# Score products of a 32-head attention on 64-row tiles of the TensorE array instead of all 128 rows with zeros

## The chip, the core and the metric

The kernel runs on one core of a Trainium2 chip. The core has a TensorE (PE in the profile) that multiplies matrices, a VectorE (DVE), a ScalarE (ACT), a GpSimd (POOL) and a SyncE (SP), which here only issues transfers. The engines run side by side, each through its own queue in order, and wait for each other on semaphores. TensorE works in two instructions: a weight load (LDWEIGHTS, engine "PEld" in the profile) puts one operand into the array, and a matmul (MATMUL, "PE") streams the other operand through it, a column at a time, into PSUM. The array has 128 rows, over which the product is summed, and 128 columns; an instruction can also be addressed to a part of it, called a tile, for which the program gives a size (rows by columns) and a position.

The metric is the device time of one execution in microseconds (us); less is better.

## What is computed

Two transformer layers on an input of 4 x 512 x 512, each an attention and a feed-forward part with layer norms and residuals. The change touches the attention of layer 0:

```python
NUM_HEADS, HEAD_DIM = 32, 16          # HIDDEN = 512, one key/value head for all query heads
q = (hidden_states @ Wq).reshape(b, s, NUM_HEADS, HEAD_DIM)
kv = hidden_states @ Wkv
k, v = (kv[..., :HEAD_DIM], kv[..., HEAD_DIM:])
scores = jnp.einsum('bqhd,bkd->bhqk', q, k) * scale
bias = slopes[:, None, None] * (pos[None, None, :] - pos[None, :, None])
scores = jnp.where(causal[None, None], scores + bias[None], -jnp.inf)
attn = jax.nn.softmax(scores, axis=-1)
out = jnp.einsum('bhqk,bkd->bqhd', attn, v).reshape(b, s, h)
return out @ Wo
```

After it come a quantized linear layer, a second attention (32 heads of 128, 8 key/value heads, rotary positions) and a feed-forward part with octonion products. The change does not touch these.

## The kernel before

The program has three stages on one core. Stage A is the attention of layer 0 with, woven into it, the projections, the layer norms and the quantized linear layer that follow it (classes `A1` and `A2`). Stage B is the second attention (`phase_b`), stage C the last feed-forward part (`C`). The matmuls at lines 422 to 483 lie in stage A alone; the last of them starts at 670 us of 2411.6.

Products of float32 precision are made from pieces: every operand is split into a rounded part h and a rest l, both of the type float32r, and three products hh, hl, lh are summed (`mm3_gen`, lines 159 to 161). For the scores of layer 0 the three products fit into one contraction, since a head has only 16 dimensions. One head takes 64 rows: 16 rows q_h against k_h, 16 rows q_l against k_h, 16 rows q_h against k_l, and 16 rows for the position bias, the block mask and, in row 58, the row maximum. Two heads share the 128 rows:

- `QS[m]` (m = 0 to 3, eight heads each) is 128 x 4 x 512. Rows 0 to 63 hold four heads, rows 64 to 127 four others (`two` = 0 and 1 in the code).
- `KS[b]` (one for each batch b) is 128 x 2 x 512. Copy `two` = 0 holds the keys in rows 0 to 63 and zeros in rows 64 to 127; copy `two` = 1 the other way round. A product over all 128 rows with copy `two` gives the scores of the head in that half; the zeros take the other head out.

The softmax is done in two passes over the scores. In the first, `max_tile` (lines 409 to 433) computes scores with 128 queries as output rows and up to 512 keys as columns, and the DVE takes the negative row maximum (line 430) into `mn`. Line 422 makes the first query block of two heads at once: it streams both copies of `KS` (2 x 128 keys) against weights from all 128 rows of `QS`. Line 426 makes one head's query block 1, 2 or 3 with 256, 384 or 512 keys. `max_end` transposes `mn` (line 439) and sends the maxima into row 58 (and 122) of `QS` by DMA (line 446). In the second pass, `exp_tile` (lines 449 to 473) computes the scores again, transposed, with 128 keys as output rows and four heads x 128 queries as columns (line 467); the ACT takes the exponential (line 470), the POOL clears what lies above the diagonal (line 472). `pv` multiplies by the values (line 483): its four matmuls for four heads go to column tiles of 32 columns each, 128 rows x 32 columns at column 0, 32, 64 and 96, in float32, which the profile shows as two instructions each (x8 for four).

The score matmuls write into few buffers: three PSUM banks `ps` (`psS`) for the maxima and two `pt` (`psT`) for the exponentials; two more banks `mm` serve the projections. A matmul waits until the DVE or the ACT has read the bank it writes.

`run` (line 561) goes over 128 units u; in unit u it records the three or four maxima matmuls of head u % 8, and the exponentials of unit u - 12, with other work (generators that are stepped in between: `front`, `qproj`, `o_piece`, `posts` of `A2`). The order in which the instructions are issued is not the recorded one: a scheduler that runs at build time and estimates durations arranges them, with the exponentials raised in priority by 100. It is thus built anew when an instruction is changed.

Two other matmuls of stage A use a part of the array: the bias row of the linear layer (line 818, two rows, `matmul(y, one, b0)`, tile of 32 rows x 128 columns, float32r) and the transpose of a 32-row tile (line 354). The transpose of the maxima at line 439 has a tile of 128 rows x 32 columns at column 0.

Of the kernel before, what the change touches and what calls it, by code (L numbers as in the profile page):

```python
# [215 lines left out]
class A1:  # L216
# [192 lines left out]
    def max_tile(self, b, m, j, q):  # L409

        nc = self.nc
        two, pr = j // 4, j % 4
        ks = self.KS[b]
        if j == 0 and q == 0:
            assert (b, m) in self.queries
            self.mn = self.sm.tile([128, 8, 4], F32, name="mn", tag="mn", bufs=2)
        ps = self.psS.tile([128, 512], F32, name="ps", tag="ps")
        qs = self.QS[m][:, pr]
        todo = []
        if q == 0 and j < 4:  # L420
            p = ps[:, 256:512].rearrange("p (i t) -> p i t", i=2)
            nc.tensor.matmul(p, qs[:, :128], ks[:, :, :128], start=True, stop=True)
            todo += [(j, 0, p[:, 0]), (j + 4, 0, p[:, 1])]
        qb = q + 1
        p = ps[:, :128 * (qb + 1)]
        nc.tensor.matmul(p, qs[:, bass.ts(qb, 128)], ks[:, two, :128 * (qb + 1)], start=True, stop=True)  # L426
        for jj, qb, p in todo + [(j, qb, p)]:
            nk = 128 * (qb + 1)
            jk = self.jp.tile([128, 512], BF, name="jk", tag="jk")
            nc.vector.tensor_tensor_reduce(  # L430
                out=jk[:, :nk], in0=p, in1=self.c.mask[:, 384 - 128 * qb:512],
                scale=-1.0, scalar=3e38, op0=ALU.add, op1=ALU.min,
                accum_out=self.mn[:, jj, qb:qb + 1])
# [15 lines left out]
    def exp_tile(self, v, q):  # L449

        nc, c = self.nc, self.c
        b, m, two, kb = v // 32, v // 8 % 4, v // 4 % 2, v % 4
        qb = kb + q
        if qb > 3:
            return
        ks = self.KS[b][:, two]
        if qb == 3:
            self.exped = v + 1
        if q == 0:
            assert v < self.maxed  # L460
            self.pe[v] = self.pp.tile([128, 4, 512 - 128 * kb], F32, name="pe", tag=f"pe{kb}")
        self.turn = (self.turn + 1) % 5
        if self.u >= 32 * B + 2 and self.turn < 3:
            ps = self.psS.tile([128, 512], F32, name="ps", tag="ps").rearrange("p (h t) -> p h t", h=4)
        else:
            ps = self.psT.tile([128, 4, 128], F32, name="pt", tag="pt")
        nc.tensor.matmul(ps, ks[:, bass.ts(kb, 128)], self.QS[m][:, :, bass.ts(qb, 128)],  # L467
                         start=True, stop=True)
        e = self.pe[v][:, :, bass.ts(q, 128)]
        nc.scalar.activation(e, ps, AF.Exp)  # L470
        if q == 0:
            nc.gpsimd.affine_select(out=e, in_=e, pattern=[[0, 4], [1, 128]], compare_op=ALU.is_ge,  # L472
                                    fill=0.0, base=0, channel_multiplier=-1)
# [921 lines left out]
```

## Time and profile before

| | |
|---|---|
| median of 3 runs | 2411.65 us (2411.24 to 2412.7) |
| the profiled execution's own time | 2413.31 us |
| its span from first to last instruction | 2411.6 us |
| mean granted TensorE clock | 0.981 of full speed |

| engine | busy us of the span | share | instructions |
|---|---|---|---|
| PE (matmul) | 2301.8 | 95% | 11606 |
| PEld (weight load) | 1794.2 | 74% | 11606 |
| DVE | 1573.0 | 65% | 4631 |
| ACT | 1076.9 | 45% | 2404 |
| POOL | 1190.3 | 49% | 1387 |

The matmuls of lines 422, 426 and 467 are 64, 384 and 320 in number; line 483 has 1024 recorded. Busy time of a PE row runs from the moment the matmul is issued to its modelled end, so rows of successive matmuls overlap, and a start-to-start distance tells more of the cost of one matmul than its duration does. The time that a matmul waits for its operands or its bank is shown as idle time of PEld or PE before it, with the instruction that ended the wait. "issue" there means that nothing in the profile explains the wait. The granted clock is what the TensorE's throttle let through, as a share of full speed.

### The profile page before, as it was taken

What the parts mean: (1) busy time and instruction counts of PE and PEld (TensorE: products, weight loads), DVE (VectorE), ACT (ScalarE), POOL (GpSimd) and SP (SyncE); (2) the same over time, 40 slices, a digit from 0 to 9 for tenths busy, and PEclk for the clock granted to TensorE, in tenths of its full rate; (3) what the DMA queues carried; (4) which work ended last, traced back from release to release, by engine and by line L of the source; (5) the groups of instructions that cost most, each with busy time, mean ns of one, the idle gap of its engine ahead of it and who ended that gap; (6) DMA issues with size and microseconds to landing.
All of it is one profiled execution on the core that took longest, in us unless ns stands there. A gap on an engine that the chain in (4) does not pass through costs nothing.

```text
span 2411.6 us, 35873 instructions
## 1 busy us (share of the span) xinstructions
PE 2301.8 (95%) x11606; PEld 1794.2 (74%) x11606; DVE 1573.0 (65%) x4631; ACT 1076.9 (45%) x2404; POOL 1190.3 (49%) x1387
## 2 busy tenths in 40 slices
PE   6899889988889999999999999999999999999998
PEld 4566455555557788888888888888888888878886
DVE  7766656555356777777777767777777778764443
ACT  3555445545543344444444444444444445453332
POOL 3323333434343676566566566666656667522221
PEclk8899899999999999999999999999999999999999
DMA  8845434343367432233122222232222222041000
GB/s 183 238 145 181 98 92 111 89 106 110 94 188 207 135 103 75 88 101 102 66 88 105 70 88 97 79 106 70 88 97 79 91 85 79 14 127 57 31 27 18
DMA packets 158558, 241.54 MB, mean 100 GB/s; under 512 B 26738, under 2 KB 91506, under 8 KB 149540
## 3 DMA queue, kind: packets, MB, share of 16 engines
q1 hardware_dynamic: 141748, 202.42, 27.9%
q0 software_dynamic: 14768, 35.92, 5.3%
q8 instruction: 93, 1.52, 0.3%
q10 hardware_dynamic: 1856, 0.92, 0.2%
q14 instruction: 93, 0.76, 0.1%
HBM read 183.17 MB, written 63.92 MB: 102 GB/s over the span
## 4 chain that ended last, share of the span: by engine, by line
PE 84%; issue 4%; DMA 4%; DVE 3%; POOL 2%; ACT 2%; SPq 1%; ACTq 0%; POOLq 0%; DVEq 0%
PE mm L182 11%; PE mm L184 11%; PE mm L183 11%; PE pt L989 6%; PE mm L159 3%; PE pt L467 3%; PE po L483 3%; PE po L1002 3%; PE po L1003 3%; PE mm L161 3%; PE po L1004 3%; PE mm L160 3%; PE ps L969 3%; PE ps L970 3%; PE ps L971 3%
## 5 line engine op out<-in xcount | busy, mean ns | idle before, releaser
L980 POOL TENSOR_TENSOR s<-s,r 128x384 f32<-128x384 f32 (+3 forms) x512 | 359.6, 722 | 130.0 <-DVE r L979 119.7
L977 ACT ACTIVATE s<-s,mn 128x384 f32<-128x384 f32 (+3 forms) x512 | 286.0, 560 | 223.8 <-DVE mn L973 215.9
L863 POOL TENSOR_TENSOR rp_a<-rp_a,rp_b 128x512 f32<-128x512 f32 x155 | 200.3, 1292 | 262.3 <-DVE rp_b L862 247.5
L992 ACT CAST ph<-pt 128x512 fp32r<-128x512 f32 x320 | 181.7, 586 | 295.5 <-PE pt L989 287.8
L430 DVE CUSTOM_DVE_ANT_0 jk<-ps,mask 128x384 bf16<-128x384 f32 (+3 forms) x512 | 227.5, 483 | 81.2 <-PE ps L426 72.1
L993 DVE TENSOR_TENSOR pl<-pt,ph 128x512 fp32r<-128x512 f32 x320 | 216.5, 686 | 43.4 <-ACT ph L992 40.4
L973 DVE CUSTOM_DVE_ANT_0 s<-ps,mask 128x384 f32<-128x384 f32 (+2 forms) x384 | 203.1, 552 | 37.7 <-PE ps L971 19.5
L470 ACT ACTIVATE pe<-pt 128x512 f32<-128x512 f32 x307 | 174.4, 600 | 97.0 <-PE pt L467 92.7
L989 PE MATMUL pt<-ident,s 128*128 128x128 f32 x1280 | 214.1, 272 | 0.7 <-POOL s L980 0.5
L182 PE MATMUL mm<-xh,w_h 128*128 128x512 f32 x512 | 205.4, 401 | 2.1 <-DVE rp_b L862 1.9
L182 PE MATMUL mm<-w_h,oh 128*128 128x512 f32 x512 | 203.7, 398 | 0.7 <-ACT oh L1008 0.7
L184 PE MATMUL mm<-xh,w_l 128*128 128x512 f32 x512 | 203.6, 398 | 0.0
L183 PE MATMUL mm<-xl,w_h 128*128 128x512 f32 x512 | 202.1, 395 | 0.0
L183 PE MATMUL mm<-w_l,oh 128*128 128x512 f32 x512 | 201.7, 394 | 0.0
L184 PE MATMUL mm<-w_h,ol 128*128 128x512 f32 x512 | 200.3, 391 | 0.0
L989 PEld LDWEIGHTS pt<-ident,s 128*128 128x128 f32 x1280 | 164.7, 140 | 46.1 <-POOL s L980 1.1
L865 POOL TENSOR_TENSOR ql<-rp_a,qh 128x512 fp32r<-128x512 f32 x124 | 160.5, 1294 | 49.6 <-ACT qh L864 49.6
L472 POOL TENSOR_SCALAR_AFFINE_SELECT pe<-pe 128x512 f32<-128x512 f32 x128 | 82.5, 647 | 195.7 <-ACT pe L470 195.1
L859 DVE TENSOR_TENSOR rp_a<-mm,cosq 128x512 f32<-128x512 f32 x128 | 88.4, 691 | 119.6 <-PE mm L184 94.3
L426 PE MATMUL ps<-KS,QS 128*128 128x256 f32 (+2 forms) x384 | 132.7, 384 | 19.2 <-DVE mn L430 18.7
L108 POOL TENSOR_TENSOR ln_rs<-ln_ve,mhalf 128x1 f32<-128x1 f32 x112 | 63.8, 575 | 173.0 <-DVE ln_ve L106 145.5
L1008 ACT CAST oh<-po 128x512 fp32r<-128x512 f32 x128 | 74.5, 582 | 166.1 <-PE po L1004 165.9
(359 smaller groups left out, 5872.5 us busy)
## 6 DMA issues: line engine op xcount, KB each, us to landing
xh<-xt SPq DMA_DIRECT2D x32, 1024.0 KB
xl<-xt SPq DMA_DIRECT2D x32, 1024.0 KB
vh<-v SPq DMA_DIRECT2D x32, 256.0 KB
vl<-v SPq DMA_DIRECT2D x32, 256.0 KB
raw<-in_a_wo SPq DMA_DIRECT2D x32, 256.0 KB
w_h<-in_a_wo POOLq DMA_DIRECT2D x32, 256.0 KB, 3.2
m_d<-t_d SPq DMA_DIRECT2D x192, 42.5 KB
QS<-qh_d SPq DMA_DIRECT2D x62, 128.0 KB
```

The source lines that it names most:

```text
L182: nc.tensor.matmul(ps, lh(k), rh(k), start=(j == 0), stop=False)
L183: nc.tensor.matmul(ps, lh(k), rl(k), start=False, stop=False)
L184: nc.tensor.matmul(ps, ll(k), rh(k), start=False, stop=(j == n - 1))
L430: nc.vector.tensor_tensor_reduce(out=jk[:, :nk], in0=p, in1=self.c.mask[:, 384 - 128 * qb:512], scale=-1.0, scalar=3e38, op0=ALU.add, op1= ...
L470: nc.scalar.activation(e, ps, AF.Exp)
L863: eng.tensor_tensor(a, a, r, ALU.add)
L973: nc.vector.tensor_tensor_reduce(out=s[:, :nk], in0=ps[:, :nk], in1=mask, scale=-1.0, scalar=3e38, op0=ALU.add, op1=ALU.min, accum_out=mn)
L977: nc.scalar.activation(s[:, :nk], s[:, :nk], AF.Exp, bias=mn, scale=-1.0, accum_out=l)
L980: nc.gpsimd.tensor_tensor(s[:, :nk], s[:, :nk], r.to_broadcast([128, nk]), ALU.mult)
L989: nc.tensor.transpose(pt[:, j], PS[u, qb, j][:, bass.ts(kb, 128)], c.ident)
L992: nc.scalar.copy(ph, pt)
L993: nc.vector.tensor_tensor(pl, pt, f(ph), ALU.subtract)
```

## The change

The score matmuls of lines 426 and 467 contract over the 64 rows that hold something, instead of over all 128. Both operands are cut to rows 64 x `two` to 64 x `two` + 63, and the matmul is addressed to the array's tile of 64 rows x 128 columns at row 0 or row 64. That makes 704 matmuls, 352 in each half. Line 422, whose weights hold two heads, stays on 128 rows. No instruction is added or taken away, the shapes of outputs, the buffers and the order in which the program records its instructions stay the same; the scheduler arranges them anew.

```diff
@@ max_tile
         qb = q + 1
         p = ps[:, :128 * (qb + 1)]
-        nc.tensor.matmul(p, qs[:, bass.ts(qb, 128)], ks[:, two, :128 * (qb + 1)], start=True, stop=True)
+        rows = slice(64 * two, 64 * two + 64)
+        nc.tensor.matmul(p, qs[rows, bass.ts(qb, 128)], ks[rows, two, :128 * (qb + 1)],
+                         start=True, stop=True, tile_position=(64 * two, 0))
         for jj, qb, p in todo + [(j, qb, p)]:
@@ exp_tile
-        nc.tensor.matmul(ps, ks[:, bass.ts(kb, 128)], self.QS[m][:, :, bass.ts(qb, 128)],
-                         start=True, stop=True)
+        rows = slice(64 * two, 64 * two + 64)
+        nc.tensor.matmul(ps, ks[rows, bass.ts(kb, 128)], self.QS[m][rows, :, bass.ts(qb, 128)],
+                         start=True, stop=True, tile_position=(64 * two, 0))
         e = self.pe[v][:, :, bass.ts(q, 128)]
```

In the issue order of the built programs, up to the last matmul of line 483, the tile size changes from one matmul to the next 299 times before the change and 598 times after it. The 704 matmuls then stand in 253 groups with no matmul of another tile size in between: 81 groups of one, 51 of two, 40 of three, 26 of four, 39 of five and 16 of six to eight. Of the 451 neighbours within a group, 350 lie in the same half of the array and 101 in different halves.

## The prediction

> **What bounds the kernel now.** I first read the page's shares and the chain that ended last, to see which engine sets the end.
>
> ```profile
> span 2411.6 us, 35873 instructions
> PE 2301.8 (95%) x11606; PEld 1794.2 (74%) x11606; DVE 1573.0 (65%) x4631; ACT 1076.9 (45%) x2404; POOL 1190.3 (49%) x1387
> PE 84%; issue 4%; DMA 4%; DVE 3%; POOL 2%; ACT 2%; SPq 1%; ACTq 0%; POOLq 0%; DVEq 0%
> ```
>
> TensorE is the chain for 84% of the span. The change lies in stage A, so I read the busy time of three stretches of it.
>
> ```profile
> 100.00:300.00 200.00, 186.15 (x1046) 118.16 (x1045) 127.77 (x502) 106.63 (x203) 62.00 (x80) 0.96 0.54 151
> 300.00:500.00 200.00, 179.40 (x971) 115.73 (x971) 116.85 (x466) 95.26 (x169) 72.53 (x107) 0.96 0.41 98
> 500.00:700.00 200.00, 177.06 (x943) 111.34 (x942) 98.06 (x348) 98.92 (x176) 76.55 (x107) 0.95 0.41 125
> ```
>
> The columns are the stretch, its length, busy PE, PEld, DVE, ACT, POOL, then granted clock, DMA share and GB/s. PE is busy for 542.6 of 600 us; the next engine, DVE, for 342.7. So PE sets the pace of stage A too, with some waits for others. What PE time is added here mostly reaches the end, since stage B can't start before it and is PE-bound itself. The question is then only what the 704 matmuls cost PE.
>
> **What a matmul costs on part of the rows.** No 64-row tile stands in this trace. The nearest row is line 818: same type float32r, same 512 columns, on a tile of 32 rows, between matmuls on all rows. This is the timeline of PE there (start, duration, engine, line).
>
> ```profile
> 375.39 0.39 PE L160 MATMUL mm<-w_l,x1h 128*128 128x512 f32 x1
> 375.62 0.39 PE L161 MATMUL mm<-w_h,x1l 128*128 128x512 f32 x1
> 375.93 0.50 PE L818 MATMUL mm<-b,one 2*128 2x512 f32 x1
> 376.36 0.50 PE L467 MATMUL pt<-QS,KS 128*128 128x512 f32 x1
> 376.79 1.06 PE L483 MATMUL po<-pe,vx 128*32 128x512 f32 x8
> ```
>
> Read the distances between starts. L160 to L161 is 0.23 us: 512 columns in a stream. L161 to L818 is 0.31 (the median of the 13 such steps in the trace's start times is 0.318): the tile size changes, and the load waits until L161 is through, 0.09 more. L818 to L467 is 0.43: again 0.09 for leaving, and 0.11 because its weight load started with it (durations 0.50 against 0.39). Without both, L818 takes the same 0.23 as 128 rows do. So fewer rows save nothing by themselves, and **a change of row tile costs 0.09 us for emptying the array plus 0.11 us for a load that no matmul covers**, 0.20 in all.
>
> A change of tile size isn't always dear:
>
> ```profile
> 413.37 0.39 PE L161 MATMUL mm<-wo_h,otl 128*128 128x512 f32 x1
> 413.60 0.27 PE L439 MATMUL mm<-ident,mn 128*32 128x128 f32 x1
> 413.62 0.48 PE L467 MATMUL pt<-QS,KS 128*128 128x512 f32 x1
> 413.94 0.28 PE L422 MATMUL ps<-KS,QS 128*128 128x256 f32 x1
> ```
>
> L439 is a transpose on 128 rows and 32 columns at column 0. It enters 0.23 after L161, as if nothing changed, and L422 starts 0.34 after it; a whole-array transpose and L467 would take 0.11 and 0.23, the same. So this change of column tile is free, and the change of rows at L818 is not. I take L818's price for 64 rows, because there as here the rows differ, and keep L439's price, zero, as the lower bound. The Trainium skill ("TensorEngine Tiling (Array Packing)", Key Properties) says that changing the tiling mode drains the TensorE. By that rule L439 would pay too; the row contradicts it, so the rule alone would not decide. By the rule every one of the added changes pays.
>
> **The sum, part by part.** Removed: nothing in number; the 704 matmuls keep their 0.23, 0.17 or 0.12 us for 512, 384 and 256 columns (start-to-start medians 0.232, 0.178 and 0.120).
>
> Added: changes of tile size. The built order has 598 against 299, so 299 more. Line 422 alone, left on 128 rows in the midst of them, stands in front of a 64-row matmul 64 times. Emptying: 299 x 0.09 = 26.9 us. Uncovered loads of 128 columns: arrivals at a tile of 128 columns go from 161 to 454 (253 at 64 rows, 185 at 128 rows, 16 at 32 rows), 293 x 0.108 = 31.6 us (0.108 is the step from 0.228 to 0.336, the common distance after a change). Arrivals at L483's 32 columns go from 138 to 144 leaving L439 in, whose load is short: nothing. Together **58.5 us** of PE time.
>
> What covers it: where PE waits anyway, an emptied array costs nothing. These are the waits at the weight load in 100 to 700 us:
>
> ```profile
> PEld ps L426 <- DVE mn L430: 31.1, 53, 6.5
> PEld pt L467 <- ACT pe L470: 22.1, 46, 1.1
> ```
>
> In the order of the trace, with lines 426 and 467 taken as 64-row tiles, 205 places would change newly; summed over them, the distance beyond streaming covers 6.1 of 40.6 us, 15%. Some later waits of these two kinds will shrink too, since DVE and ACT, busy 57% and 50%, lose nothing and get more time between matmuls. I take 20% covered; bounds are none and half. On the path: 0.8 x 58.5 = 46.8 us; bounds 29.3 and 58.5.
>
> Gained: overlap of the two halves. The row nearest to it is L483: its four column tiles run together, eight instructions of 512 columns in 1.06 us, where eight in a row would take 8 x 0.23 = 1.83. Within the 253 groups I let each half start when it is free and in order: of 140.0 us of streaming (448 x 0.229 + 128 x 0.174 + 128 x 0.118) 15.6 us then overlap, so little because 350 of 451 neighbours are of the same half. With the same 0.8 for waits: 12.5 us; bounds 0 and 15.6. TensorE: Matmul & The Clock Gate (Part 3, Measured speedup vs the span model), a page of the Trainium skill, gives 2.38 to 3.07 times for three or four tiles together; if every head's matmul found a partner, 70 us would go, an estimate from that page that this order doesn't allow.
>
> A cost I leave at zero: weight loads between neighbours of the same half. In the whole-array stream the load of the next matmul is hidden, and on L483's tiles all eight loads start within the first pass:
>
> ```profile
> 403.58 0.16 PEld L483 LDWEIGHTS po<-pe,vx 128*32 128x32 f32 x8 [0.24 <-issue]
> 403.58 0.85 PE L483 MATMUL po<-pe,vx 128*32 128x384 f32 x8
> ```
>
> Eight loads in 0.16 us, four of them for tiles still streaming. The same page (What overlaps and what doesn't) says a load overlaps a running matmul only where the row group differs; this row and the stream speak against it. If it held, 350 neighbours x 0.108 = 37.8 us would come on top.
>
> The scheduler's new order adds little by itself: with the old order the count would be 580 instead of 598, 18 x 0.2 = 3.6 us of the sum. No DMA is added; those into `QS` (line 446) wait for the maxima as before and move with them.
>
> Net: 46.8 - 12.5 = +34.3 us, all in stage A. The profiled execution took 2413.31 with its span of 2411.6, so 1.7 us lie around the span; the median without the profiler is 2411.65, to which I add: **2446 us**. Bounds: 29.3 - 15.6 = +13.7 (2425) and +58.5 (2470).
>
> **The rivals.**
> - *Loads of the same half don't overlap.* For: no 64-row pair is in the trace. Against: the two rows above. 34.3 + 0.8 x 37.8 = +65: 2476; without any overlap of halves 2489.
> - *Free change, faster.* Going to a row half costs what L439 shows, nothing, and the overlap stays: -15.6, so 2396. For: L439. Against: all of L818's steps. It decides when a change costs under 15.6 / 299 = 0.052 us.
> - *Waits cover it.* If 75% of the 58.5 fell into PE's waits and all overlap came, 14.6 - 15.6 = -1: 2411. Against: PE's own idle time before L426 and L467 in this stage is only some 20 us.
> - *The clock.* Half-filled rows could count as less activity, and the granted 0.96 of these stretches fall, say to 0.85: 600 x (0.96 / 0.85 - 1) = +78, with the changes 2524. Nothing in the rows shows it: L483 and L818 run without such a fall.
>
> **How the numbers follow.** Forecast 0.74; loads exposed 0.08; free change 0.09; covered 0.06; clock 0.03. The forecast's own range is 2425 to 2470. To leave out no more than two in ten I widen it for what the sum can't know (a new order of waits, part of the first rival): 2417 to 2478. A difference under 0.2% (4.8 us) can't be told from no change; faster than that 0.09, within it 0.06, slower 0.85.
>
> **What would show it.** Starts 0.32 apart before a 64-row matmul that follows a 512-column one on all rows, and 0.34 behind it; starts a few ns apart for neighbours in different halves; 0.23 between neighbours in the same half; the weight loads' idle time put to "issue" before the score matmuls and what follows them growing by tens of us; stage B beginning about 34 us later and lasting as long. The forecast fails if 64-row tiles enter at 0.23, or if waits for DVE and ACT in stage A fall by as much as the changes cost.

## The result and the profile after

The changed kernel takes 2501.39 us (median of 4 runs, 2497.57 to 2521.14), the kernel before, run beside it, 2411.44 us. The ratio is 1.0384, 95% interval 1.0359 to 1.041: 90 us slower, where 34 were forecast.

The page of the kernel after (busy time, the chain, and the granted clock in 40 slices):

```profile
span 2498.9 us, 35870 instructions
PE 2398.5 (96%) x11606; PEld 1809.2 (72%) x11606; DVE 1576.6 (63%) x4631; ACT 1082.3 (43%) x2404; POOL 1191.4 (48%) x1387
PEclk8799788888789999999999999999999999999999
PE 86%; issue 4%; DVE 3%; DMA 2%; ACT 2%; POOL 2%; SPq 0%; ACTq 0%; POOLq 0%; DVEq 0%
```

The clock row of the kernel before, for comparison:

```profile
PEclk8899899999999999999999999999999999999999
```

PE is the chain as before and is busy for 97 us more. What is new is the clock row: slices 5 to 12, the attention of layer 0, now have 7 and 8 where they had 8 and 9. The same three stretches of stage A as in the prediction, after the change (stretch, length, busy PE, PEld, DVE, ACT, POOL, granted clock, DMA share, GB/s):

```profile
100.00:300.00 200.00, 193.58 (x946) 105.99 (x948) 114.92 (x451) 97.06 (x184) 52.92 (x66) 0.88 0.49 144
300.00:500.00 200.00, 184.02 (x847) 103.53 (x839) 103.28 (x417) 85.40 (x148) 62.04 (x92) 0.85 0.29 78
500.00:700.00 200.00, 183.77 (x800) 105.48 (x801) 98.17 (x378) 85.62 (x149) 65.03 (x93) 0.80 0.30 89
```

PE is as busy as before, but does fewer matmuls in the same time (2593 instead of 2960), and the clock is 0.80 to 0.88 instead of 0.95 to 0.96. Stage B begins with its first key projection at 813.5 us instead of 727.8: 85.7 of the 87.3 us of the span are lost before it.

At the full clock, PE's timeline of the kernel after shows the price of the changes of tile as it was read from line 818:

```profile
486.15 0.60 PE L147 MATMUL mm<-ident,po_ot 128*128 128x128 f32 x4
486.68 0.50 PE L821 MATMUL mm<-b,one 2*128 2x512 f32 x1
487.11 0.38 PE L427 MATMUL ps<-KS,QS 64*128 64x256 f32 x1
487.33 0.39 PE L470 MATMUL pt<-QS,KS 64*128 64x512 f32 x1
487.64 1.06 PE L486 MATMUL po<-pe,vx 128*32 128x512 f32 x8
...
489.70 0.38 PE L422 MATMUL ps<-KS,QS 128*128 128x256 f32 x1
490.02 0.38 PE L427 MATMUL ps<-KS,QS 64*128 64x256 f32 x1
490.33 0.50 PE L159 MATMUL mm<-wo_h,oth 128*128 128x512 f32 x1
490.66 0.40 PE L160 MATMUL mm<-wo_l,oth 128*128 128x512 f32 x1
```

L422 (128 rows) to L427 (64 rows) to L159 (128 rows): 0.32 and 0.31 us for 256 columns that stream in 0.12, and 0.33 instead of 0.23 from L159 on. In the start times of the whole trace, a 512-column matmul on all rows is followed by a 64-row one, at the full clock, after 0.319 us in the median of 47, against the 0.318 of line 818.

At the low clock, the same work looks like this:

```profile
450.48 0.79 PE L470 MATMUL pt<-QS,KS 64*128 64x512 f32 x1
450.48 0.90 PE L427 MATMUL ps<-KS,QS 64*128 64x256 f32 x2
451.18 0.62 PE L470 MATMUL pt<-QS,KS 64*128 64x512 f32 x1
451.74 1.08 PE L486 MATMUL po<-pe,vx 128*32 128x256 f32 x8
452.75 1.01 PE L427 MATMUL ps<-KS,QS 64*128 64x512 f32 x2
```

Single 512-column matmuls last 0.62 instead of 0.39. The first two lines also show the overlap of two halves: both start at 450.48.

The waits of the weight loads, kernel after (total us, times, longest):

```profile
PEld ps L427 <- DVE mn L432: 27.0, 41, 2.4
PEld pt L470 <- ACT pe L473: 22.3, 41, 1.2
PEld ps L427 <- issue: 21.3, 60, 1.7
PEld pt L470 <- issue: 19.2, 50, 1.7
```

and kernel before:

```profile
PEld ps L426 <- issue: 6.2, 13, 1.2
PEld pt L467 <- issue: 5.9, 15, 1.7
```

Waits for DVE and ACT are nearly what they were (31.1 and 22.1); "issue" grew from 12 to 40 us on these two lines. I take that for the emptying of the array: in the kernel before, all idle time ahead of line 818 (5.2 us in 16 waits) is put to "issue" too.

To add this up I split every distance between two matmul starts from 97 us (the first product with the values) to the start of stage B: streaming at the full clock (medians by columns, 0.229 for 512); up to 0.09 for leaving a tile size and 0.108 for arriving at one with 128 columns; up to as much streaming again where the low clock is recorded; and the rest, called waits. A wait that falls on a change of tile is booked as tile change first. All in us:

| kernel | streaming | tile changes | low clock | waits | sum |
|---|---|---|---|---|---|
| before | 469.2 | 41.7 | 21.2 | 98.4 | 630.5 |
| after | 462.8 | 87.8 | 76.0 | 89.7 | 716.3 |
| difference | -6.4 | +46.1 | +54.8 | -8.7 | +85.8 |

So two things of about equal size make the loss: the tile changes, as forecast, and the clock. The split is my reading of start times; the runs below take up the two parts.

### The profile page after: what moved, and what is told of

The parts are those of the page before. It is cut to its first block, busy times and chain, and to the rows that moved or that the text cites. A ratio compares the mean times of both kernels' runs of the same rounds, so it can differ in the third digit from the quotient of the medians.

```text
span 2498.9 us, 35870 instructions
## 1 busy us (share of the span) xinstructions
PE 2398.5 (96%) x11606; PEld 1809.2 (72%) x11606; DVE 1576.6 (63%) x4631; ACT 1082.3 (43%) x2404; POOL 1191.4 (48%) x1387
## 4 chain that ended last, share of the span: by engine, by line
PE 86%; issue 4%; DVE 3%; DMA 2%; ACT 2%; POOL 2%; SPq 0%; ACTq 0%; POOLq 0%; DVEq 0%
PE mm L182 10%; PE mm L184 10%; PE mm L183 10%; PE pt L992 5%; PE po L486 4%; PE ps L427 4%; PE pt L470 4%; PE mm L159 3%; PE mm L161 3%; PE mm L160 3%; PE po L1006 3%; PE po L1005 3%; PE po L1007 3%; PE ps L972 3%; PE ps L973 3%
## 5 line engine op out<-in xcount | busy, mean ns | idle before, releaser
L427 PE MATMUL ps<-KS,QS 64*128 64x256 f32 (+2 forms) x384 | 153.8, 451 | 12.8 <-DVE mn L432 12.4
L470 PE MATMUL pt<-QS,KS 64*128 64x512 f32 x307 | 149.4, 513 | 4.3 <-DMA QS<-mt 2.0
```

What stands on the lines that cost most here:

```text
L427: nc.tensor.matmul(p, qs[rows, bass.ts(qb, 128)], ks[rows, two, :128 * (qb + 1)], start=True, stop=True, tile_position=(64 * two, 0))
L470: nc.tensor.matmul(ps, ks[rows, bass.ts(kb, 128)], self.QS[m][rows, :, bass.ts(qb, 128)], start=True, stop=True, tile_position=(64 * two, 0))
```

## The experiments

Two theories. R: work on half of the rows counts as half for the granted clock, so that stretches rich in it stay at the low clock, and the tile changes cost their 0.2 us besides. S: the tile changes are all, and their idle time is what brings the clock down.

### Streams of matmuls by themselves

Three of the seven stretches (`ops` picks a bank, one of four weights and the streamed operand; `gap` lets the DVE work for some 14 us before the next operand is ready):

```diff
+        xr = gap(1)
+        for i in range(300):
+            nc.tensor.matmul(*ops(xr, i, A), start=True, stop=True, tile_position=(0, 0))
+        xr = gap(2)
+        for i in range(100):
+            nc.tensor.matmul(*ops(xr, i, FULL), start=True, stop=True)
+        for i in range(300):
+            nc.tensor.matmul(*ops(xr, i, A), start=True, stop=True, tile_position=(0, 0))
+        xr = gap(3)
+        for i in range(300):
+            o = 64 * (i % 2)
+            nc.tensor.matmul(*ops(xr, i, slice(o, o + 64)), start=True, stop=True, tile_position=(o, 0))
...
```

> The kernel computes nothing of the reference: it streams matmuls of float32r, 512 columns each, in seven stretches, each after some 14 us in which TensorE waits: 300 on all rows; 300 on rows 0 to 63; 100 on all rows and then 300 on rows 0 to 63; 300 on the two halves in turn; 240 on all rows and on rows 0 to 63 in turn; the same after 100 on all rows; 240 on all rows and on a small 32-row tile in turn. Theory R (work on half of the rows counts as half for the clock): the second stretch never reaches the full clock, its matmuls stay 0.43 us apart as in cold stretches of the profiles, while the first falls to 0.23 after some microseconds; the third keeps 0.23, since the clock was already full; the fourth is full again, with 0.11 to 0.12 us a matmul. Theory S (only the emptied array costs, its idle time lowers the clock): the second and third stretches warm up and run at 0.23 like the first; the clock falls in the fifth and seventh. Both: a pair of one 128-row and one 64-row matmul takes 0.23 + 0.23 + 2 x 0.20 = 0.86 us at full clock.

Measured in one run, one stretch of steady work out of each, in order (length, busy PE with the number of matmuls, PEld, DVE, POOL, granted clock, DMA share, GB/s):

```profile
35.00:85.00 50.00, 50.00 (x222) 41.39 (x221) 0.00 (x0) 0.00 (x0) 1.00 0.00 1
110.00:230.00 120.00, 120.00 (x282) 92.28 (x282) 0.00 (x0) 0.00 (x0) 0.50 0.00 0
282.00:340.00 58.00, 58.00 (x258) 47.08 (x257) 0.00 (x0) 0.00 (x0) 1.00 0.00 1
365.00:390.00 25.00, 25.00 (x224) 23.59 (x223) 0.00 (x0) 0.00 (x0) 1.00 0.01 1
412.00:580.00 168.00, 168.00 (x233) 66.39 (x233) 1.71 (x3) 0.00 (x0) 0.50 0.00 0
625.00:718.00 93.00, 93.00 (x219) 40.22 (x218) 0.00 (x0) 0.00 (x0) 1.00 0.00 0
740.00:855.00 115.00, 115.00 (x221) 62.68 (x221) 0.00 (x0) 0.00 (x0) 0.50 0.00 0
```

Length by number gives the time of a matmul. All rows: 50 / 222 = 0.23 at clock 1.00. The same on 64 rows, begun after a pause: 120 / 282 = 0.43, at clock 0.50 to its last matmul, though TensorE never waits. The same again, begun while the clock was high: 0.23 (third line). The two halves in turn: 0.11, two at a time, and the clock rises. This is theory R's picture and excludes S for the second stretch, which has no change of tile at all. The fifth and seventh lines add something that R did not say and S did: with a change of tile after every matmul the clock does not rise either, in the seventh without any half rows. And it holds the high clock when it begins with it (sixth line, 93 x 2 / 219 = 0.85 a pair; 0.86 was expected from line 818's price). So the clock has two marks, one for rising and a lower one for falling. What is held against them below is a share: the part of the time in which columns are streamed, each matmul counted by its rows out of 128.

### Where the marks lie

> Computes nothing of the reference. Five stretches of float32r matmuls of 512 columns, each after a wait of TensorE of some 14 us: 2, 4 and 8 matmuls on all rows to 1 on rows 0 to 63; 300 on all rows with rows 64 to 127 of the streamed operand zero; 100 on all rows and then 300 on 32 rows. If the clock rises on the share of time in which rows are streamed, a half-row matmul counting half, the shares at the low clock are (2 x 0.427 + 0.213) / 1.87 = 0.57, (4 x 0.427 + 0.213) / 2.73 = 0.70 and (8 x 0.427 + 0.213) / 4.44 = 0.82; in the changed kernel's trace windows that rose had 0.67 or more and windows that stayed low up to 0.77, so the first stays low, the third rises, the second decides. Zeros count as rows: the fourth rises to 0.23 us a matmul. If instead the data count (zeros as idle), it stays at 0.43 like the half-row stretch. 32 rows count a quarter, 0.25 x 0.94 = 0.23, at or below the shares at which windows of the changed kernel fell (0.34 and less): the fifth falls to 0.43 some microseconds after the 32-row matmuls begin; if not, falling needs real idleness.

The kernel has the same form with other stretches, and ran once too. In its first stretch (two on all rows to one on 64) the matmuls stay 0.624 us apart on average, 1.87 for three. That is the sum at the low clock: 3 x 0.427, and 0.59 for two changes of tile, as in a pair of the fifth stretch above (168 x 2 / 233 = 1.44). The clock's record begins only behind this stretch. The others:

```profile
185.00:245.00 60.00, 60.00 (x195) 33.33 (x195) 0.00 (x0) 0.00 (x0) 1.00 0.00 0
272.00:325.00 53.00, 53.00 (x197) 35.05 (x197) 0.00 (x0) 0.00 (x0) 1.00 0.00 0
355.00:410.00 55.00, 55.00 (x244) 45.54 (x243) 0.00 (x0) 0.00 (x0) 1.00 0.00 1
465.00:578.00 113.00, 113.00 (x266) 85.85 (x265) 0.00 (x0) 0.00 (x0) 0.50 0.00 0
```

The first line is four to one, share 0.70: the clock rises. The second is eight to one: it rises too. The third has zeros in rows 64 to 127 of the streamed operand: 0.23 us, full clock. So rows count that an instruction addresses, not what lies in them. The zeros of the kernel before will have kept its clock up in the same way; at line 426 they lie in the streamed operand, at line 467 in the weights, which no stream tried. The last line, on 32 rows, fell to 0.43 us after beginning at the full clock. The mark for rising thus lies between shares of 0.57 and 0.70. Falling happens at 0.23 (32 rows) and not at 0.47 (64 rows: 0.427 / 2 of streaming in every 0.227, halved), nor at 0.38, the share of the sixth stretch above, which held the high clock: (0.213 + 0.107) / 0.853.

### Tile changes without half-row work

```diff
+        if q == 0:
+            nc.tensor.matmul(ps[:, 0, 0:2], ks[0:32, bass.ts(kb, 128)], self.QS[m][0:32, 0, 0:2],
+                             start=True, stop=True, tile_position=(0, 0))
         nc.tensor.matmul(ps, ks[:, bass.ts(kb, 128)], self.QS[m][:, :, bass.ts(qb, 128)],
                          start=True, stop=True)
```

> The kernel before, with a 32-row matmul of 2 columns put ahead of each first exponential matmul (128 of them, overwritten by the matmul behind it): 554 changes of tile size instead of 299, and no streaming on half of the rows. Theory R: 255 x 0.20 x 0.8 = +41 us, 2452, with the granted clock about as before (0.975 to 0.981). Theory S: emptying brings the clock down as in the changed kernel, where 299 changes went with 55 us of lost clock, so 41 + 47 = +88, 2500, clock 0.955 or lower.

Measured 2451.27 us (2448.92 to 2453.8) against 2411.25 beside it, ratio 1.0156 (1.0134 to 1.0178), mean clock 0.981. Stage A's stretches:

```profile
100.00:300.00 200.00, 189.59 (x1016) 120.88 (x1016) 120.20 (x466) 101.03 (x189) 55.28 (x72) 0.97 0.50 140
300.00:500.00 200.00, 181.50 (x965) 114.82 (x966) 116.31 (x470) 91.01 (x161) 69.13 (x102) 0.97 0.35 91
500.00:700.00 200.00, 179.56 (x918) 111.34 (x916) 91.30 (x335) 94.41 (x167) 72.34 (x103) 0.93 0.34 99
```

The clock column is that of the kernel before within 0.02. 255 changes cost 40.0 us, 0.157 each, 0.79 of the 0.198 read from line 818; the 128 added matmuls themselves are in it. That is near the forecast's term with its 0.8, measured without the clock. Theory S falls in the kernel itself: nearly as many changes as the whole change adds leave the clock where it was. From 97 us to the start of stage B the low clock is recorded for 54.6 us here, and for 54.6 in the kernel before.

### One of the two edits alone

On the kernel before, max64 has only the first edit and exp64 only the second:

```diff
-        nc.tensor.matmul(p, qs[:, bass.ts(qb, 128)], ks[:, two, :128 * (qb + 1)], start=True, stop=True)
+        rows = slice(64 * two, 64 * two + 64)
+        nc.tensor.matmul(p, qs[rows, bass.ts(qb, 128)], ks[rows, two, :128 * (qb + 1)],
+                         start=True, stop=True, tile_position=(64 * two, 0))
```

```diff
-        nc.tensor.matmul(ps, ks[:, bass.ts(kb, 128)], self.QS[m][:, :, bass.ts(qb, 128)],
-                         start=True, stop=True)
+        rows = slice(64 * two, 64 * two + 64)
+        nc.tensor.matmul(ps, ks[rows, bass.ts(kb, 128)], self.QS[m][rows, :, bass.ts(qb, 128)],
+                         start=True, stop=True, tile_position=(64 * two, 0))
```

> Only the maxima on 64 rows. The built order has 781 changes of tile size, more than the whole change (598), but 384 matmuls on 64 rows instead of 704, 59 us of streaming instead of 140. Theory R: 482 x 0.2 x 0.8 = 77, and of the clock's 55 us the share of the half-row work, some 25: 2512. Theory S: 77 + 55 x 482 / 299 = 77 + 89: 2577. If changes cost little and half-row streaming is all: 2411 + 25 = 2436.

> Only the exponentials on 64 rows: 731 changes of tile size, 320 matmuls on 64 rows, 73 us of streaming. Theory R: 432 x 0.2 x 0.8 = 69, and 29 for the clock: 2509. Theory S: 69 + 79: 2559. If only half-row streaming counts: 2440.

The maxima alone stream for 67 us (140 less 73); the 59 in the expectation of max64 is wrong.

| kernel | us | ratio (95%) | tile changes, built order | 64-row matmuls | mean clock | low clock from 97 us to stage B, us |
|---|---|---|---|---|---|---|
| max64 | 2489.97 | 1.0328 (1.0285 to 1.0371) | 781 | 384 | 0.974 | 85.3 |
| exp64 | 2495.55 | 1.0343 (1.0317 to 1.0369) | 731 | 320 | 0.969 | 112.6 |
| after | 2501.39 | 1.0384 (1.0359 to 1.041) | 598 | 704 | 0.951 | 198.0 |

One line of each, 300 to 500 us, max64 and then exp64:

```profile
300.00:500.00 200.00, 185.54 (x843) 101.84 (x842) 104.25 (x418) 84.56 (x147) 61.02 (x91) 0.92 0.29 74
```

```profile
300.00:500.00 200.00, 185.43 (x835) 103.50 (x834) 101.33 (x398) 84.09 (x144) 61.64 (x90) 0.88 0.28 77
```

The clock goes by the half-row work and not by the number of changes: with 781 changes it is 0.92 here, with 598 and all of the half-row work 0.85. In the split used above, against the kernel before, max64 has +88.0 for tile changes, +10.8 for the clock and -26.5 in waits, exp64 +83.3, +20.9 and -26.8. Both came out 22 and 13 us below what theory R gave (2512 and 2509), and farther from S (2577 and 2559) and from half-row streaming alone (2436 and 2440). In the split more of the changes found cover in waits than the 0.2 that I kept, and half of the half-row work costs less than half of the clock's loss, 10.8 and 20.9 alone against 54.8 together. That fits marks rather than a rate, but was not tested further.

### Fewer changes, more half-row work

```diff
-        if q == 0 and j < 4:
-            p = ps[:, 256:512].rearrange("p (i t) -> p i t", i=2)
-            nc.tensor.matmul(p, qs[:, :128], ks[:, :, :128], start=True, stop=True)
-            todo += [(j, 0, p[:, 0]), (j + 4, 0, p[:, 1])]
+        if q == 0:
+            p = ps[:, 256:384]
+            rows = slice(64 * two, 64 * two + 64)
+            nc.tensor.matmul(p, qs[rows, :128], ks[rows, two, :128], start=True, stop=True,
+                             tile_position=(64 * two, 0))
+            todo += [(j, 0, p)]
```

> The changed kernel with line 422 also on 64 rows, one head at a time (64 matmuls of 256 columns become 128 of 128): 525 changes of tile size instead of 598, 832 matmuls on 64 rows. Theory R: against the kernel before 226 x 0.2 x 0.8 = 36 for the changes, the same 55 as in the changed kernel for the clock, 9 less in waits and 8 less by overlap: 2411 + 74 = 2485; the clock stays near 0.95. If the loss of clock followed the number of changes: 36 + 55 x 226 / 299 - 17 = 61, 2472.

Measured 2490.56 us (2483.95 to 2493.69), ratio 1.0318 (1.0297 to 1.034), clock 0.951. The split gives +29.1 for tile changes, +59.3 for the clock, -9.5 in streaming and -4.4 in waits. A quarter of the added changes went, and with them some 11 us; the clock's loss stayed, with 208.2 us at the low clock. 2490.56 is nearer to R's 2485 than to 2472.

### The opposite on the kernel before

```diff
-        self.b0 = wp.tile([2, 512], F32R, name="b0")
-        self.one = wp.tile([2, 128], F32R, name="one")
+        self.b0 = wp.tile([128, 512], F32R, name="b0")
+        self.one = wp.tile([128, 128], F32R, name="one")
+        nc.gpsimd.memset(f(self.b0), 0.0)
...
-        nc.vector.tensor_scalar(self.one, c.ident[0:2], 0.0, 1.0, ALU.mult, ALU.add)
+        nc.vector.tensor_scalar(self.one, c.ident, 0.0, 1.0, ALU.mult, ALU.add)
...
-        split(nc, hi, self.b0, raw, nc.gpsimd)
+        split(nc, hi, self.b0[0:2], raw, nc.gpsimd)
```

> The opposite of the change on the kernel before: the bias row of line 818 goes over all 128 rows, 126 of them zero, instead of a tile of 32 rows. 282 changes of tile size instead of 299 up to the last matmul of line 483. Theory R: 16 matmuls, each with two changes fewer where matmuls on all rows stand around it: at most 16 x 2 x 0.2 = 6.4 us, with 0.8 on the path 5: 2406. If changes of 32-row tiles cost nothing on the path: 2411, no difference.

Measured 2408.45 us (11 runs, 2404.36 to 2412.93) against 2412.82 (15 runs), ratio 0.9983 (0.9974 to 0.9992): 4.4 us faster, 5 expected. Putting zeros under a small matmul, to keep it in the tile of its neighbours, beats the kernel before by 0.17%. Whether the changes alone did it is not shown: the low clock is also shorter in this trace, 41.0 us instead of 54.6.

## Why the prediction was wrong

**Right.**
- *Fewer rows save nothing by themselves.* 64-row and 128-row streams both run at 0.227 us a matmul at the full clock.
- *The price of a change.* 0.319 on the way in, where line 818 showed 0.318, and 0.85 a pair alone in a stream, 0.86 expected.
- *The tile-change term.* 46.8 us forecast with the cover taken off; in the split of the changed kernel +46.1, and 37.4 with the 8.7 us by which the waits shrank, within the bounds of 29.3 and 58.5. tiny32 measures price times cover, 0.79 against the 0.8 taken; that it comes so near is in part luck, since its 128 added matmuls are in it and max64 and exp64 found more cover.
- *Loads between neighbours of the same half cost nothing.* 0.227 in the third stretch of the streams; the rival of 2476 had no ground.
- *Free changes, or changes covered by waits.* Neither rival came: waits shrank by only 8.7 us, and a change costs what it did at line 818.

**Off in size.** Overlap of the halves: 12.5 us forecast, 6.4 fewer in streaming. Of the 101 neighbours in different halves 52 start within 10 ns of each other; of the others 37 start 0.2 us or more apart (in 12 of them the one issued second starts first), so far that little or nothing is left for the two to overlap. Alone, halves in turn do overlap fully (0.11 a matmul).

**The step that failed** is the one that left the clock out of the sum: "Half-filled rows could count as less activity, and the granted 0.96 of these stretches fall, say to 0.85 ... Nothing in the rows shows it: L483 and L818 run without such a fall", priced at +78 and given 0.03. It came, with 0.80 to 0.88, and cost 54.8 us in the split; the forecast's 34 with it makes 89, and 90 was measured. That this fits so well is in part luck: without the clock the split has 46.1 - 8.7 - 6.4 = 31.0 us, where the changes, some 9 us too dear in the forecast, and the overlap, 6 us too large, nearly cancel. The two rows that I set against it could not speak: L818 is 0.43 us long, while the low stretches of the clock's record last 3.4 us or multiples of it, and L483's tiles have 32 columns but all 128 rows. What did speak was the clock column itself, 0.95 to 0.96 in these stretches and 1.00 in stage B: stage A already fell below the mark at times, so work that counts half could be expected to keep it there. In the kernel before the low clock is recorded for 55 us between 97 us and stage B, in the one after for 198.

How it comes about, from the records of the changed kernel in windows of 3.4 us: the 16 windows in which the clock fell had row-weighted streaming shares of 0.06 to 0.34, and the 16 from which it rose 0.67 to 1.00. The kernel before has 12 falls, at waits of the stage. Of the 16, about half are new in kind: in them the array streamed for 0.4 to 0.64 of the window, more than in any fall of the kernel before (0.37 at most), and only the weighting by rows brings the share so low. After a fall the half-row matmuls and the emptied array keep the share below the rising mark, and the clock stays low for 14 to 27 us in nine of the 16 times, where in the kernel before it recovered after 3.4 in nine of 12. That it is the rows can be read here too: of the 42 windows that stayed low, some 18 would have a share of 0.80 or more without the weighting, as much as windows that rose. The Trainium skill (TensorE: Matmul & The Clock Gate, Part 1, What's actually happening) describes a gate that passes 4 or 8 of 8 pulses by how busy TensorE was in windows of 3.4 us; the records here agree, with 0.5 and 1.0 as their only values. That rows are weighed is what the streams show.

**Open.** Whether the changed kernel would gain just those 55 us at the full clock was not tried in the kernel itself: filling the idle half needs PSUM banks, and all eight are in use. Windows that stayed low reach up to 0.77, above the 0.70 at which a steady stream rose, and some that kept the high clock come down to 0.23 to 0.35, depending on how long a transpose is taken to stream; how the share is taken over time I can't tell. Each variant was also scheduled anew, so no run holds the issue order fixed; the counts of changes and the split stand for what the order does. The rates for one edit alone (10.8 and 20.9) against both are explained by marks, not measured as such.

## What to carry to other kernels

A tile of fewer rows saves no time by itself: it pays only where matmuls of different halves are issued next to each other, ready at the same time, in groups long enough to carry 0.2 us for each change of tile size. Rows filled with zeros count as work for the clock and rows left out do not, so before making a matmul smaller read the clock column of its stage: if it is already below 1.00, less activity can cost as much again as the tile changes, here 55 us beside 46. A small matmul in the midst of full ones was here a little cheaper padded to their tile, 4.4 us for 16 of them.

## What the runs showed of the hardware that I had not expected

- The granted clock weighs work by the rows addressed, whatever they hold: an unbroken stream on 64 rows stayed at 0.50 after a pause, one on 128 rows with 64 of them zero in the streamed operand rose to 1.00.
- It has two marks. Rising took a share of more than 0.57 and at most 0.70 in steady streams, falling came at 0.23 and not at 0.38; a 64-row stream ran at 0.23 or 0.43 us a matmul for all of its 300 matmuls, depending on how it began.
- Two halves of the array run a float32r matmul each at the same time for the price of one (0.11 us a matmul). The gain of up to two-fold that the Trainium skill gives for 64-row tiles (TensorEngine Tiling (Array Packing), Theoretical Speedup) is thus real in a stream, and 6 of 140 us in this kernel.
